# More turns between routing's top-k scans and around the recurrence's scan, in a two-layer macaron network with mixture of experts

## The chip, the cores and the metric

One core of a Trainium2 chip. The metric is the device time of one execution in microseconds (us), as the median of several executions. The profile is of one more execution.

## The reference, cut to what matters

The input is 16 sequences of 512 tokens with 128 channels. Six residual steps follow one another; each begins with a layer norm:

```
x = x + 0.5 * kan(norm(x))            # 64 inner units, each a sum of 16 relus
x = x + attention(norm(x))            # 16 heads of 8 channels, causal
x = x + 0.5 * kan(norm(x))
x = x + 0.5 * moe(norm(x))            # first pass over the experts, k = 0
x = x + recurrence(norm(x))
x = x + 0.5 * moe(norm(x))            # second pass, k = 1
```

The experts' step lets each of 8 experts choose its 128 best tokens of each sequence:

```
probs = softmax(x @ gate.T)                    # per token, over 8 experts
g, m  = top_k(probs of one sequence and expert over its 512 tokens, 128)
h     = gelu(x[m] @ w1[e]) @ w2[e]             # 128 -> 512 -> 128
out[m] += g * h
```

The recurrence is a gated linear scan over the 512 tokens with 64 states, `s = lam * s + u`, with `lam` from two sigmoids and `u` from a linear map of the normed input, and a linear map of the state and of the input back to 128 channels.

## The kernel before, in words

All residuals stay in on-chip memory (tiles `x0` to `x15`). The order of the instructions on TensorE (PE), VectorE (DVE), ScalarE (ACT) and GpSimd (POOL) is that of the program text as it runs: each engine takes its own instructions in that order and waits for what each needs. The text is a set of Python generators. One call of `turn()` advances every live generator to its next `yield`. So a `yield` means: let the others put their instructions in before mine go on. "A turn" below is one such round. It has no length of its own; it only fixes the order.

The first 1000 us are attention, the relu sums and the first scores, sequence by sequence. Then `hurry` is set, the pacing by budgets ends, and three things run beside one another:

- `experts()` (from L835) takes one job, a sequence and an expert, per three turns. A job's first product (`ps_h`, L879) stands in the first turn, its second (`ps_y`, L894) some turns later. For half of the experts the result is added back by a product with a selection matrix (`acc`, L912), which needs three DVE operations (L891, L903, L900); for the others GpSimd scatters it to memory (L926). If the next job's tokens have not been moved yet (`begun[0] < moved[0]` fails), the loop goes through its three turns without a new job.
- `fetch()` (L796) lets GpSimd gather the tokens of one job per turn (L805), in the order of `order`: 256 jobs, products and scatters mixed, of two passes. It stops at a job whose group of sequences has not been routed. `dispatch()` (L812) transposes gathered tokens on PE two jobs at a time (L827) and copies them.
- `recurrences()` waits until both sequences of a pair have come back from the first pass, then runs `recurrence(pair)` (L981): norms, transposes (L288), products, DVE's scan (L1010), the output products of both sequences (`leave`, L1017 and L1018), the residual add (L1023), and `gated(1, b)`, which norms again and computes scores (L692). A norm goes from DVE's statistics (L257, L261) to GpSimd's reciprocal root (L263, L264) back to DVE's normalisation (L274).

`routing(k, g)` (L700) starts when the eight sequences of group g have scores for pass k. It turns scores into probabilities, transposes them (L726), and then finds the 128 best of 512 for all 64 rows at once, eight per round: sixteen rounds of three DVE operations (`max` L738, `max_index` L740, `match_replace` L742). Each of these scans reads all 512 scores. After them the token numbers are converted and transposed (L749, L753, L754), copied (L756 to L758), and the group counts as routed. Of its four runs, (0,0) lies in the first 1000 us; (0,1), (1,0) and (1,1) run beside the experts. `if not hurry[0]` at L744 gives the first run three further turns after each scan; the others have one turn per scan.

The conditions that hold the gathers and the transposes:

```
while (k, g) not in routed or i >= moved[0] + 2 * E or ...:   # fetch
    yield
while i + 1 >= fetched[0] or i > begun[0] + AHEAD:            # dispatch, i even
    yield
```

Of the kernel before, what the change touches and what calls it, by code (L numbers as in the profile page):

```python
# [44 lines left out]
def tile_macaron(  # L45
# [51 lines left out]
    with ExitStack() as ph:  # L97
# [102 lines left out]
        def need(**work):  # L200
            while paced[0] and any(w > room[e] for e, w in work.items()):
                yield
            for e, w in work.items():
                room[e] -= w
# [10 lines left out]
        def rest(turns):  # L215

            for _ in range(turns if hurry[0] else 0):
                yield
# [3 lines left out]
        def bank(shape, dtype, name, work=0.0):  # L222


            while held[0] == 2 or (paced[0] and work > room["pe"]):
                yield
            room["pe"] -= work
            held[0] += 1
            return mm.tile(shape, dtype, name=name, tag="mm")

        def freed():
            held[0] -= 1

        def together(*gs):

            got, live = [None] * len(gs), list(enumerate(gs))
            while live:
                left = []
                for i, g in live:
                    try:  # L240
                        next(g)
                        left.append((i, g))
                    except StopIteration as end:
                        got[i] = end.value
                live = left
                if live:
                    yield
            return got
# [437 lines left out]
        def gated(k, b):  # L686

            xn, xT = yield from norm(x[b], whole=True)
            nc.sync.dma_start(out=xnd[b].rearrange("(c p) d -> p c d", p=P), in_=xn)
            ps = yield from bank([P, NT, E], F32, "ps_g", 0.9)  # L690
            for c in range(NT):
                nc.tensor.matmul(ps[:, c, :], lhsT=xT[:, bass.ts(c, P)], rhs=gateT, start=True, stop=True)  # L692
            yield
            take(dve=0.2)
            nc.vector.tensor_copy(scores[b // GB][:, :, b % GB, :], ps)
            freed()
            scored[k] += 1
            yield

        def routing(k, g):  # L700


            while scored[k] < (g + 1) * GB:
                yield
            N = GB * E
            sc3 = scores[g].rearrange("p c b e -> p (c b) e")
            mx = rtp.tile([P, NT * GB], F32, name="mx")
            probs = rtp.tile([P, NT, N], F32, name="probs")
            pr3 = probs.rearrange("p c (b e) -> p (c b) e", e=E)
            wide = [P, NT * GB, E]  # L710
            nc.vector.tensor_reduce(mx, sc3, AX.X, ALU.max)
            nc.vector.tensor_sub(pr3, sc3, mx.unsqueeze(2).to_broadcast(wide))
            yield
            nc.scalar.activation(pr3, pr3, AF.Exp)
            yield
            yield
            sm = rtp.tile([P, NT * GB], F32, name="sm")
            nc.vector.tensor_reduce(sm, pr3, AX.X, ALU.add)
            nc.vector.reciprocal(sm, sm)
            nc.vector.tensor_mul(pr3, pr3, sm.unsqueeze(2).to_broadcast(wide))  # L720
            yield
            yield
            yield from rest(2)
            ps = yield from bank([N, NT, P], F32, "ps_p")
            for c in range(NT):
                nc.tensor.transpose(ps[:, c, :], probs[:, c, :], ident)  # L726
            yield
            wk = rtp.tile([N, S], F32, name="wk")
            nc.vector.tensor_copy(wk, ps.rearrange("n c q -> n (c q)"))
            freed()  # L730
            gain = rtp.tile([N, CAP], F32, name="gain")
            tok = rtp.tile([N, CAP], U32, name="tok")
            for i in range(CAP // 8):
                m8 = gain[:, bass.ts(i, 8)]
                for op in range(3):
                    yield from need(dve=0.75)
                    if op == 0:
                        nc.vector.max(out=m8, in_=wk)  # L738
                    elif op == 1:
                        nc.vector.max_index(tok[:, bass.ts(i, 8)], m8, wk)  # L740
                    else:
                        nc.vector.match_replace(out=wk, in_to_replace=m8, in_values=wk, imm_value=-1.0)  # L742
                    yield
                    if not hurry[0]:  # L744
                        yield
                        yield
                        yield
            tokf = rtp.tile([N, CAP], F32, name="tokf")
            nc.vector.tensor_copy(tokf, tok)  # L749
            yield  # L750
            yield from rest(2)
            ps = yield from bank([P, 2, N], F32, "ps_r")
            nc.tensor.transpose(ps[:, 0, :], tokf, ident[0:N, 0:N])  # L753
            nc.tensor.transpose(ps[:, 1, :], gain, ident[0:N, 0:N])  # L754
            yield
            nc.vector.tensor_copy(tokI[g], ps[:, 0, :])  # L756
            nc.vector.tensor_copy(tokT[g], ps[:, 0, :])
            nc.vector.tensor_scalar_mul(gainT[g], ps[:, 1, :], 0.5)  # L758
            freed()
            routed.add((k, g))  # L760
            yield
# [219 lines left out]
        def recurrence(pair):  # L981
            half = [slice(a * M, (a + 1) * M) for a in range(2)]
            rows = (2 * pair, 2 * pair + 1)
            xTs = yield from together(*(norm(x[b], f"rope_{'ab'[a]}", w1p, True) for a, b in enumerate(rows)))
            xTs = [xT for _, xT in xTs]

            pf = yield from bank([P, S], F32, "ps_f")
            for a in range(2):
                nc.tensor.matmul(pf[half[a], :], lhsT=wf, rhs=xTs[a], start=True, stop=True)
            yield  # L990
            fg = w2p.tile([P, S], F32, name="fg", tag="kan_s")
            nc.scalar.activation(fg, pf, AF.Tanh, scale=0.5)
            freed()
# [3 lines that stand above are left out]
            pl = yield from bank([P, S], F32, "ps_l")  # L997
            nc.tensor.matmul(pl, lhsT=wlam, rhs=fg, start=True, stop=True)
            yield
            lam = w2p.tile([P, S], F32, name="lam", tag="oT")  # L1000
            nc.scalar.activation(lam, pl, AF.Tanh, bias=lbias, scale=0.25)
            freed()
            yield
            nc.vector.tensor_scalar(lam, lam, 0.5, 0.5, ALU.mult, ALU.add)
            pu = yield from bank([P, S], F32, "ps_u")
            for a in range(2):
                nc.tensor.matmul(pu[half[a], :], lhsT=wb, rhs=xTs[a], start=True, stop=True)
            yield
            s = w2p.tile([P, S], F32, name="s", tag="y")
            nc.vector.tensor_tensor_scan(s, lam, pu, 0.0, ALU.mult, ALU.add)  # L1010
            freed()
            yield

            def leave(a, b):
                po = yield from bank([P, NT, D], F32, "ps_h2")
                for c in range(NT):
                    nc.tensor.matmul(po[:, c, :], lhsT=xTs[a][:, bass.ts(c, P)], rhs=wx, start=True, stop=False)  # L1017
                    nc.tensor.matmul(po[:, c, :], lhsT=s[half[a], bass.ts(c, P)], rhs=wc[half[a], :],  # L1018
                                     start=False, stop=True)
                    if c == 1:  # L1020
                        yield
                yield
                nc.vector.tensor_add(x[b], po, x[b])  # L1023
                freed()
                yield
                yield from gated(1, b)

            yield from together(*(leave(a, b) for a, b in enumerate(rows)))

        def recurrences():  # L1030
            while scored[0] < B:
                yield
            for pair in range(B // 2):
                while done[0] < 2 * pair + 2:
                    yield
                yield from recurrence(pair)
# [128 lines left out]
```

## Time and profile before

| | us |
|---|---|
| median of 3 runs | 1751.41 |
| lowest, highest | 1749.4, 1756.8 |
| the profiled execution | 1746.91 |
| its span, first to last instruction | 1745.2 |
| mean granted clock of TensorE | 0.971 |
| routing's three scans of the 16 rounds, mean of one (L738, L740, L742) | 0.68, 0.68, 0.67 |
| the recurrence's scan (L1010), mean of one | 1.22 |
| an expert's gather on GpSimd (L805), mean of one | 0.98 |
| an expert's scatter on GpSimd (L926), mean of one | 1.62 |

The views: the page gives busy times of the engines over the whole span. A table of stretches gives the same for parts of it, with the clock that the throttle granted to TensorE. The timeline of one engine lists its instructions in order: start, duration, operation, output and inputs, and in brackets the idle time before it and who ended that. A row can merge several instructions of one kind; the time is then that of all. Ends of matrix products are modelled, so a busy TensorE is not one at full rate. Lines are those of the kernel before.

### The profile page before, as it was taken

What the parts mean: (1) busy time and instruction counts of PE and PEld (TensorE: products, weight loads), DVE (VectorE), ACT (ScalarE), POOL (GpSimd) and SP (SyncE); (2) the same over time, 40 slices, a digit from 0 to 9 for tenths busy, and PEclk for the clock granted to TensorE, in tenths of its full rate; (3) what the DMA queues carried; (4) which work ended last, traced back from release to release, by engine and by line L of the source; (5) the groups of instructions that cost most, each with busy time, mean ns of one, the idle gap of its engine ahead of it and who ended that gap; (6) DMA issues with size and microseconds to landing.
All of it is one profiled execution on the core that took longest, in us unless ns stands there. A gap on an engine that the chain in (4) does not pass through costs nothing. (4 is left out here: it accounts for less than half of the span.)

```text
span 1745.2 us, 35245 instructions
## 1 busy us (share of the span) xinstructions
PE 1636.9 (94%) x12879; PEld 1111.0 (64%) x12879; DVE 1107.3 (63%) x3604; ACT 996.6 (57%) x2000; POOL 977.6 (56%) x1453
## 2 busy tenths in 40 slices
PE   6788999999999999899899899999999999999997
PEld 2334444444444444444444389899988889989997
DVE  6677767777787788788876137643467444672222
ACT  3445667777777776677667654344443334444443
POOL 2524535545565455455534767567663777647773
PEclk9889999999999999999999899999998999999999
DMA  4211111011110111011122113233322233323342
GB/s 117 76 52 36 44 44 43 28 42 51 54 37 32 42 55 47 16 48 54 35 70 63 31 44 73 51 64 73 62 60 45 55 73 63 66 56 71 68 82 48
DMA packets 101753, 94.77 MB, mean 54 GB/s; under 512 B 11859, under 2 KB 90140, under 8 KB 101340
## 3 DMA queue, kind: packets, MB, share of 16 engines
q1 hardware_dynamic: 74512, 67.45, 12.5%
q0 software_dynamic: 26048, 24.93, 8.8%
q8 instruction: 101, 1.65, 0.4%
q14 instruction: 72, 0.59, 0.1%
q10 hardware_dynamic: 1020, 0.15, 0.0%
HBM read 58.93 MB, written 37.49 MB: 55 GB/s over the span
## 5 line engine op out<-in xcount | busy, mean ns | idle before, releaser
L625 ACT ACTIVATE pt<-ps_st 128x512 f32<-128x512 f32 (+1 forms) x704 | 386.9, 561 | 238.3 <-PE ps_st L622 232.9
L627 POOL TENSOR_SCALAR_AFFINE_SELECT pt<-pt 128x128 f32<-128x128 f32 (+2 forms) x704 | 247.0, 355 | 405.0 <-ACT pt L625 400.4
L569 DVE CUSTOM_DVE_ANT_0 below<-ps_sc,causal 128x512 bf16<-128x512 f32 (+1 forms) x512 | 316.5, 618 | 117.2 <-PE ps_sc L564 103.1
L881 ACT ACTIVATE mo<-ps_h 128x512 f32<-128x512 f32 x256 | 153.1, 598 | 262.2 <-PE ps_h L879 262.0
L805 POOL DMA_INDIRECT xg<-xnd,tokI x256 | 249.9, 976 | 80.5 <-issue 42.8
L879 PE MATMUL ps_h<-xin,mw 128*128 128x128 f32 x2048 | 281.1, 281 | 0.0
L894 PE MATMUL ps_y<-mw,mo 128*128 128x128 f32 x2048 | 274.7, 278 | 0.0
L564 PE MATMUL ps_sc<-kp,qp 72*128 72x512 bf16 (+3 forms) x1024 | 260.7, 307 | 10.6 <-DVE maxs L569 8.0
L622 PE MATMUL ps_st<-qp,kp 99*128 99x512 bf16 (+3 forms) x1024 | 259.8, 307 | 5.7 <-ACT pt L625 4.8
L879 PEld LDWEIGHTS ps_h<-xin,mw 128*128 128x128 f32 x2048 | 252.7, 194 | 6.3 <-issue 3.7
L926 POOL DMA_INDIRECT sum<-ye,tokI x124 | 201.3, 1624 | 97.7 <-ACT ye L897 31.2
L894 PEld LDWEIGHTS ps_y<-mw,mo 128*128 128x128 f32 x2048 | 251.7, 194 | 2.3 <-issue 1.0
L622 PEld LDWEIGHTS <-kp 99*128 99x128 bf16 x1024 | 94.2, 101 | 203.8 <-issue 185.4
L329 ACT ACTIVATE kan_h<-kan_s,rbias,kw 128x512 f32<-128x512 f32 x256 | 206.6, 814 | 7.1 <-PE ps_kg L335 6.9
L574 DVE TENSOR_REDUCE maxs<-ps_sc 128x2 f32<-128x512 f32 (+1 forms) x192 | 130.6, 685 | 70.5 <-PE ps_sc L564 69.3
L335 PE MATMUL ps_kg<-kan_h,w2d 128*64 128x512 f32 x512 | 164.7, 640 | 3.1 <-ACT kan_h L329 3.0
L645 PE MATMUL ps_av<-pt,va 128*32 128x512 f32 (+3 forms) x2048 | 166.8, 444 | 0.0
L564 PEld LDWEIGHTS <-qp 72*128 72x128 bf16 x1024 | 97.5, 100 | 55.6 <-issue 33.9
L900 DVE TENSOR_TENSOR mo<-mo 128x128 bf16<-128x128 f32 x132 | 38.3, 290 | 137.8 <-ACT mo L885 137.6
L912 PE MATMUL acc<-mo 128*128 128x128 bf16 x1584 | 113.0, 220 | 6.0 <-DVE mo L900 5.8
L912 PEld LDWEIGHTS <-mo 128*128 128x128 bf16 x1584 | 99.5, 99 | 23.8 <-issue 22.5
L645 PEld LDWEIGHTS ps_av<-pt,va 128*32 128x32 f32 x2048 | 53.6, 109 | 93.0 <-issue 49.7
(195 smaller groups left out, 2308.8 us busy)
## 6 DMA issues: line engine op xcount, KB each, us to landing
qp<-qs SPq DMA_DIRECT2D x64, 288.0 KB
xnd<-kan_x SPq DMA_DIRECT2D x32, 256.0 KB
sum<-x SPq DMA_DIRECT2D x31, 256.0 KB
qs<-qpart SPq DMA_DIRECT2D x48, 128.0 KB
kp<-ks SPq DMA_DIRECT2D x48, 96.0 KB
x<-in_L_attn_x_dram SPq DMA_DIRECT2D x16, 256.0 KB
mw<-in_L_ffn_w_dram SPq DMA_DIRECT2D x16, 256.0 KB
xg<-xnd,tokI POOLq DMA_INDIRECT x256, 2.5
```

The costliest lines, as they stand in the source:

```text
L329: nc.scalar.activation(h, sk, AF.Relu, bias=rbias[:, t : t + 1], scale=kw1[:, t : t + 1])
L564: nc.tensor.matmul(v[:, u, 0:n], lhsT=qp[r][0 : 9 * HD, g, bass.ts(c, P)], rhs=kp[0 : 9 * HD, r, 0:n], start=alone, stop=(u == len(gs) - 1 ...
L569: nc.vector.tensor_tensor_reduce(below[:, 0:n], v[:, 0, 0:n], causal[:, S - n : S], 1.0, LOWEST, ALU.add, ALU.max, accum_out=maxs[:, c, h ...
L622: nc.tensor.matmul(v[:, u, 0:n], lhsT=kp[ROWS, r, bass.ts(c, P)], rhs=qp[r][ROWS, g, c * P : S], start=True, stop=True)
L625: nc.scalar.activation(o, v[:, :, 0:n], AF.Exp, scale=HD ** -0.5)
L627: nc.gpsimd.affine_select(out=dg, in_=dg, compare_op=ALU.is_ge, fill=0.0, base=0, pattern=[[0, len(gs)], [1, P]], channel_multiplier=-1)
L645: nc.tensor.matmul(po[32 * g : 32 * g + 32, c * P : S], lhsT=va[:, c, r, :], rhs=pt[:, g, OFF[c] : OFF[c] + n], start=(c == 0), stop=(c == ...
L805: nc.gpsimd.indirect_dma_start(out=xgs[i // E % 2][:, i % E, :], out_offset=None, in_=xnd[b], in_offset=bass.IndirectOffsetOnAxis(ap=tokI[ ...
L879: nc.tensor.matmul(pst[:, f, :], lhsT=mw1[e][:, bass.ts(f, P)], rhs=xins[i // E % 2][:, i % E, :], start=True, stop=True)
L894: nc.tensor.matmul(py, lhsT=hs[u][:, f, :], rhs=mw2[e][:, f, :], start=(f == 0), stop=(f == NF - 1))
L912: nc.tensor.matmul(acc[:, c, :], lhsT=sels[u][:, bass.ts(c, P)], rhs=yes[u][:, w, :], start=(e == 0 and c == 0 and w == 0), stop=(e == las ...
L926: nc.gpsimd.indirect_dma_start(out=sums[k, b], out_offset=bass.IndirectOffsetOnAxis(ap=tokI[g][:, n : n + 1], axis=0), in_=ye[:, b % 2 * ( ...
```

## The change

Beside the experts, routing's first two scans of a round are followed by two turns each in place of one, the third by one as before: five turns for three scans. The recurrence gets one more turn before its product `ps_u`, two more after its scan, and one more after each sequence's residual add. Nothing is computed otherwise, and no tile or buffer changes.

```diff
@@ -744,6 +744,8 @@ routing
                     if not hurry[0]:
                         yield
                         yield
+                        yield
+                    elif op < 2:
                         yield
             tokf = rtp.tile([N, CAP], F32, name="tokf")
@@ -1002,6 +1004,7 @@ recurrence
             freed()
             yield
             nc.vector.tensor_scalar(lam, lam, 0.5, 0.5, ALU.mult, ALU.add)
+            yield
             pu = yield from bank([P, S], F32, "ps_u")
@@ -1009,6 +1012,9 @@
             nc.vector.tensor_tensor_scan(s, lam, pu, 0.0, ALU.mult, ALU.add)
             freed()
             yield
+
+            yield
+            yield
 
             def leave(a, b):
@@ -1022,6 +1028,7 @@
                 yield
                 nc.vector.tensor_add(x[b], po, x[b])
                 freed()
+                yield
                 yield
                 yield from gated(1, b)
```

## The prediction

> **What bounds the kernel now.** I read the page's busy shares first, then the table of stretches, then the timeline of single engines around the places where TensorE's share drops, and last the starts of each expert job.
>
> ```profile
> PE 1636.9 (94%) x12879; PEld 1111.0 (64%) x12879; DVE 1107.3 (63%) x3604; ACT 996.6 (57%) x2000; POOL 977.6 (56%) x1453
> ```
>
> TensorE is the bound. All edits take effect after 1000 us, beside the experts, so the question is where TensorE loses time there.
>
> ```profile
> 1060.00:1110.00 50.00, 44.88 (x414) 42.20 (x413) 47.62 (x141) 20.77 (x54) 32.40 (x30) 0.97 0.29 55
> 1325.00:1330.00 5.00, 5.00 (x19) 3.88 (x18) 0.62 (x1) 0.37 (x1) 0.00 (x0) 0.50 0.02 3
> 1500.00:1560.00 60.00, 56.96 (x561) 55.18 (x560) 49.10 (x135) 29.17 (x69) 33.13 (x28) 1.00 0.30 56
> 1575.00:1700.00 125.00, 125.00 (x1278) 124.66 (x1277) 35.77 (x105) 62.33 (x154) 97.42 (x83) 1.00 0.38 75
> ```
>
> Columns: stretch, its length, busy us of PE, PEld, DVE, ACT, POOL, granted clock, DMA share, GB/s. Without routing (last row) PE is full; with it (first, third row) DVE is full or nearly so and PE starves. In the second row PE counts as busy, but at half clock. The timeline of DVE and PE shows why:
>
> ```profile
> 1318.99 0.67 DVE L738 MAX8 gain<-wk 64x8 f32<-64x512 f32 x1
> 1319.59 1.19 DVE L1010 TENSOR_TENSOR_SCAN s<-lam,ps_u 128x512 f32<-128x512 f32 x1
> ```
>
> ```profile
> 1320.83 0.48 PE L1018 MATMUL ps_h<-wc,s 64*128 64x128 f32 x2 [1.91 <-DVE s L1010]
> ```
>
> The recurrence's scan stands behind routing's, its consumer is already next on PE, PE waits 1.91 us, and its clock is halved from 1322.5 to 1336.
>
> The first product of each job is a measure that half clock cannot hide. Every eighth job, in the timeline of PE:
>
> ```profile
> 1242.89 0.44 PE L879 MATMUL ps_h<-xin,mw 128*128 128x128 f32 x2
> 1264.92 0.44 PE L879 MATMUL ps_h<-xin,mw 128*128 128x128 f32 x2
> 1292.22 0.44 PE L879 MATMUL ps_h<-xin,mw 128*128 128x128 f32 x2
> 1317.59 0.44 PE L879 MATMUL ps_h<-xin,mw 128*128 128x128 f32 x2
> 1352.95 0.44 PE L879 MATMUL ps_h<-xin,mw 128*128 128x128 f32 x2
> ```
>
> These are jobs 80, 88, 96, 104 and 112. With a recurrence and no routing, eight jobs take 22.03 and the next eight 27.30 us; with routing 25.37 and 35.36. Experts alone: 18.06 (1586.83 to 1604.89).
>
> **The Trainium skill.** "TensorE: Matmul & The Clock Gate", Part 1, says that the clock falls to half after an idle window of about 3.4 us and comes back after a busy one. The trace agrees in kind: half clock lasts about 3.4 us after most gaps, but 13.65 us from 1322.5 on; even 1.98 us of waiting (at 1099.5) was enough. "DMA: Bandwidth & Descriptors", section on the SWDGE path, puts a fixed part of about 2.0 us on each transfer issued by GpSimd; the gathers here land 2.5 us after their issue (median), so I use 2.5.
>
> **Part 1: routing, what is won.** A block has 16 rounds of three scans. From 1307.73 to 1310.08 three scans and one 0.19 us operation went out, so a scan costs DVE 0.72 us. An expert job takes three turns. Three turns for three scans ask 2.16 us of DVE, beside some 0.5 for the job itself (0.75 for each second job's three operations, 0.4 for each fourth's copy, rounded up for the residual add) and, where a recurrence runs, about 0.76 (12.2 us per pair in 48 turns). PE needs 18.06/8 = 2.26 us without, 49.33/16 = 3.08 with a recurrence. So DVE is late by 0.3 to 0.4 us a job. With five turns DVE's share falls to about 1.8 of 2.26 and 2.6 of 3.08, and PE leads again.
>
> Loss against the undisturbed pace, from the job starts:
> - block (0,1), jobs 24 to 40 (1068.67, 1089.68, 1116.94): 21.01 - 18.06 + 27.26 - 22.03 = 8.2
> - block (1,0), jobs 96 to 120 (to 1376.65): 3.3 + 8.1 + (23.70 - 22.03) = 13.1, the wait for the scan and its half clock in it
> - block (1,1), jobs 160 to 184 (1508.78, 1528.71, 1549.67, 1568.77): 1.9 + 2.9 + 1.0 = 5.8
>
> That is 27; routing's own transposes, some 1.9, stay, which leaves 25. Bunches remain: eight statistics and eight normalisations put 2.2 and 2.1 us on DVE within five turns, and three or four of them fall into (1,0). I take 20 as won, bounds 14 and 25.
>
> **Part 2: the recurrence's turns.** They put one to two expert products between the scan and its consumer, which covers its 1.2 us. The gain is in the 13.1 already. In undisturbed pairs the scan ended before PE came to it (scan at 1165.70 for 1.22, consumer at 1167.53), so nothing is won there. Nothing is added but four turns until scores exist.
>
> **Part 3: what routing's delay costs.** A block's scans now need 80 turns, 26.7 jobs, in place of 48, 16 jobs. Following the generators turn by turn:
> - (0,1) starts after job 20 and ends near 48; job 59 is the first that needs it. Free.
> - (1,0) starts after job 98. Jobs from 122 on wait for it: 123 is the first of the second pass and tokens move in pairs. Before: 98 + 16 = 114, in time. After: 98 + 26.7 = 124.7, and four turns of tail: too late. Job 122 begins 15 turns late, five rounds of the expert loop issue nothing new.
> - (1,1) starts after job 162 or 163; jobs from 186 on wait. Before 178, after 190 and tail: again five empty rounds.
>
> An empty round is no fixed time: PE waits until DVE has finished, the gathers have been issued and landed.
>
> Dry spell 1, from the start of job 121's first product. Both halves of the recurrence's output (3.2 each, 1167.21 to 1170.44), a first product (0.95) and a second (0.9): x is added by 9.0. Behind that on DVE: four scans 2.9, statistics and aggregates 2.1, two expert operations 0.6 (GpSimd's two roots, 2.6, end about with them): 14.9. Normalisation 2.1, the last scan 0.75, conversions 0.4: 18.2. PE's last sum and the two small transposes: 19.1. DVE's residual add and token copy: 20. GpSimd issues the first gather 0.3 later, then one each 1.25 us:
>
> ```profile
> 1556.04 1.01 POOL L805 DMA_INDIRECT xg<-xnd,tokI  x1 [1.20 <-DVE gainT L758]
> 1557.35 1.05 POOL L805 DMA_INDIRECT xg<-xnd,tokI  x1 [0.30 <-PE ps_y L894]
> 1558.71 0.94 POOL L805 DMA_INDIRECT xg<-xnd,tokI  x1 [0.30 <-PE ps_x L827]
> ```
>
> The transposes of tokens 128 and 129 stand ahead of job 124: seven gathers, 20.3 + 7.5 + 2.5 = 30.3, job 124 at 30.6. In that time PE has 17.7 of work (recurrence 6.4, first products 2.9, second 2.7, sums 2.0, transposes 2.1, scores 1.7). Idle 12.9.
>
> Dry spell 2, from job 185. Seven scans 5.0 and 2.5 of expert and conversion work on DVE: 7.6; residual add and token copy 8.4; first gather 8.7, seventh lands at 18.7, job 188 at 19.1. PE's own work 8.7. Idle 10.4.
>
> After each, half clock for one to two windows costs 1.7 to 3.4; I take 2. Sum 14.9 + 12.4 = 27.3. Bounds 20 (DVE ahead of PE, a warm clock) and 38 (see below).
>
> One wait moves but stays: after (1,0) GpSimd works off its late gathers, and the next norm's roots stand behind them (a 2.56 us wait of PE at 1396.0, eight jobs in 32.88 for 27.30). After the change about 32 gathers, five scatters and two roots, 52 us, stand before the same norm of the next pair, which PE reaches at some 51: about the same wait. Counted at nothing, plus or minus 3. In spell 1 the gathers themselves are that queue. In (1,1) no norm follows.
>
> **Sum.** -20 + 27.3 = +7.3 us. The profiled execution took 1746.9 (span 1745.2), 4.5 below the median of 1751.4; so 1754.2 by its measure, 1758.7 by the median's.
>
> **Rivals.**
> - Not slower: the relief outweighs the dry spells. For it: DVE was over 95% busy in 1060 to 1110, so all of 25 may come back, and DVE may enter a dry spell ahead. Costs at their low end, 20: 1746; at best some 1742. Against it: both chains end in seven gathers in single file, which no faster DVE shortens. It decides where the spells together cost less than is won.
> - Clearly slower: the cold clock. If each spell is followed by 13.65 us of half clock, as at 1322.5, 6.8 in place of 2 is lost twice, and the norm's wait grows by 3: costs 38 to 40 and +18 to 20, 1770. Against it: that stretch was the recurrence's small products, while after the spells dense first and second products run.
>
> **Chances.** Forecast (+1 to +14) 0.55, 1752 to 1766 its own range; not slower 0.25, about half of it beyond 0.5%; clearly slower 0.20. Half a per cent, about what a measurement can tell from no change, is 8.8 us: faster 0.12; same 0.13 plus 0.32 of the forecast; slower 0.23 plus 0.20. Range 1744 to 1773, cutting a little from either rival.
>
> **What would show it.** Right: in the profile after, eight-job stretches of 18 and of 22 and 27 us where the scans run, no wait at the consumer of the scan, DVE below 90% there; two holes in PE of 10 to 13 us in all, one shortly before the first job of the second pass, one some 65 jobs later, each ended by a gather. Wrong: holes under 5 us, or eight-job stretches that keep their excess.

## The result, and the profile after

The median went from 1750.61 us (1746.59 to 1756.80, 20 runs) to 1757.61 us (1754.85 to 1760.54, 20 runs): a ratio of 1.0038, 95% interval 1.0030 to 1.0045, or +7.0 us for a forecast of +7.3. The profiled execution of after took 1758.35 (span 1756.6), so the two profiles are 11.4 apart in span. The profile of before was 3.7 below its kernel's median and that of after 0.7 above; the sums below are made on the two profiles and end on 11.4, not on 7.0. In after `ps_h` is L881, `ps_y` L896, `acc` L914, the gathers L807, their transposes L829, the recurrence's output L1023 and L1024.

The busy shares from the page of after:

```profile
PE 1640.2 (93%) x12879; PEld 1112.5 (63%) x12879; DVE 1108.6 (63%) x3604; ACT 1000.9 (57%) x2000; POOL 976.8 (56%) x1453
```

The work is the same to the instruction; only its order changed. From the table of stretches of after, the first and the third row for the two stretches shown of before, then the two places where scans have run out and the gathers are awaited (columns as before: stretch, length, busy us of PE, PEld, DVE, ACT, POOL, clock, DMA share, GB/s):

```profile
1060.00:1110.00 50.00, 50.00 (x488) 47.57 (x487) 43.09 (x127) 25.03 (x62) 36.71 (x34) 1.00 0.35 66
1375.00:1400.00 25.00, 18.04 (x111) 16.23 (x111) 12.88 (x62) 4.89 (x11) 16.04 (x19) 0.73 0.24 61
1500.00:1560.00 60.00, 59.40 (x597) 58.84 (x597) 41.60 (x117) 31.50 (x73) 33.45 (x27) 1.00 0.34 63
1570.00:1600.00 30.00, 23.15 (x191) 21.42 (x190) 10.62 (x33) 9.32 (x24) 20.14 (x20) 0.83 0.28 60
```

Where the scans run, PE is now full and DVE is at 86% and 69%, for 95% and 82% before. In their place stand two holes with idle time and a lowered clock. The timeline of PE through the first hole, cut to the rows that start after a wait and the first product of job 122:

```profile
1376.49 0.83 PE L914 MATMUL acc<-mo 128*128 128x128 bf16 x12
1380.53 2.37 PE L288 MATMUL ps_t<-ident,kan_x 128*128 128x128 f32 x8 [3.20 <-DVE kan_x L274]
...
1388.03 0.48 PE L829 MATMUL ps_x<-ident,xg 128*128 128x128 f32 x1 [3.23 <-DMA xg<-xnd,tokI]
1388.30 3.42 PE L692 MATMUL ps_g<-gateT,kan_xT 128*128 128x8 f32 x16
1391.58 1.84 PE L881 MATMUL ps_h<-xin,mw 128*128 128x128 f32 x7
```

And the second, in (1,1):

```profile
1579.63 0.48 PE L829 MATMUL ps_x<-ident,xg 128*128 128x128 f32 x1 [3.11 <-DMA xg<-xnd,tokI]
1581.05 0.45 PE L829 MATMUL ps_x<-ident,xg 128*128 128x128 f32 x1 [0.95 <-DMA xg<-xnd,tokI]
1582.13 0.47 PE L829 MATMUL ps_x<-ident,xg 128*128 128x128 f32 x1 [0.63 <-DMA xg<-xnd,tokI]
1582.40 1.92 PE L881 MATMUL ps_h<-xin,mw 128*128 128x128 f32 x8
```

In the first hole PE waits twice: 3.20 us for the norm of a recurrence's output, which without new expert jobs has nothing beside it to fill the time, then 3.23 us for the gather of the tokens that the late routing has only just named. In the second the waits shown are for gathers alone. The first gathers of the two holes, in GpSimd's timeline:

```profile
1385.31 1.03 POOL L807 DMA_INDIRECT xg<-xnd,tokI  x1 [2.46 <-DVE gainT L760]
1576.98 1.00 POOL L807 DMA_INDIRECT xg<-xnd,tokI  x1 [2.15 <-DVE gainT L760]
```

The job's first product at 1582.40 then runs at half clock: it takes 1.92, for 1.06 at 1568.42.

The starts of the first products give the account by stretches of jobs. (Below, "excess" is what a stretch takes over the undisturbed pace: 18.06 per eight jobs without a recurrence, 49.33 per sixteen with one.)

| jobs | us before | us after | difference | what happens there |
|---|---|---|---|---|
| 24 to 48 | 75.57 | 68.14 | -7.4 | scans of (0,1) |
| 48 to 64 | 49.33 | 56.02 | +6.7 | late gathers of (0,1) |
| 96 to 120 | 84.43 | 73.79 | -10.6 | scans of (1,0) |
| 120 to 144 | 82.80 | 98.30 | +15.5 | empty rounds of (1,0) |
| 160 to 184 | 59.99 | 55.23 | -4.8 | scans of (1,1) |
| 184 to 192 | 18.06 | 30.17 | +12.1 | empty rounds of (1,1) |
| before 24, and after the last | | | -1.5, +1.5 | |

All other stretches agree within 0.1 us. The sum is +11.5, by the unrounded numbers the 11.4 of the spans. The tail is what follows the last first product: 18.5 for 17.0. Of the -1.5 before job 24, 0.6 lies in jobs 16 to 24, where routing of (0,1) has begun, and is relief too.

### The profile page after: what moved, and what is told of

It reads as the page before. It is cut to its first block, busy times and chain, and to the rows that moved or that the text cites. A ratio compares the mean times of both kernels' runs of the same rounds, so it can differ in the third digit from the quotient of the medians.

```text
span 1756.6 us, 35232 instructions
## 1 busy us (share of the span) xinstructions
PE 1640.2 (93%) x12879; PEld 1112.5 (63%) x12879; DVE 1108.6 (63%) x3604; ACT 1000.9 (57%) x2000; POOL 976.8 (56%) x1453
## 3 DMA queue, kind: packets, MB, share of 16 engines
q1 hardware_dynamic: 74512, 67.45, 12.4%
## 5 line engine op out<-in xcount | busy, mean ns | idle before, releaser
L807 POOL DMA_INDIRECT xg<-xnd,tokI x256 | 249.1, 973 | 85.4 <-issue 45.8
L881 PE MATMUL ps_h<-xin,mw 128*128 128x128 f32 x2048 | 284.4, 283 | 0.0
L896 PE MATMUL ps_y<-mw,mo 128*128 128x128 f32 x2048 | 271.6, 276 | 0.0
L881 PEld LDWEIGHTS ps_h<-xin,mw 128*128 128x128 f32 x2048 | 256.1, 196 | 12.6 <-issue 9.9
L896 PEld LDWEIGHTS ps_y<-mw,mo 128*128 128x128 f32 x2048 | 250.2, 193 | 1.1 <-issue 0.8
L914 PE MATMUL acc<-mo 128*128 128x128 bf16 x1584 | 112.1, 220 | 1.5 <-DVE mo L893 0.5
L914 PEld LDWEIGHTS <-mo 128*128 128x128 bf16 x1584 | 99.7, 99 | 12.1 <-issue 9.2
```

The costliest lines, as they stand in the source:

```text
L807: nc.gpsimd.indirect_dma_start(out=xgs[i // E % 2][:, i % E, :], out_offset=None, in_=xnd[b], in_offset=bass.IndirectOffsetOnAxis(ap=tokI[ ...
L881: nc.tensor.matmul(pst[:, f, :], lhsT=mw1[e][:, bass.ts(f, P)], rhs=xins[i // E % 2][:, i % E, :], start=True, stop=True)
L896: nc.tensor.matmul(py, lhsT=hs[u][:, f, :], rhs=mw2[e][:, f, :], start=(f == 0), stop=(f == NF - 1))
L914: nc.tensor.matmul(acc[:, c, :], lhsT=sels[u][:, bass.ts(c, P)], rhs=yes[u][:, w, :], start=(e == 0 and c == 0 and w == 0), stop=(e == las ...
```

## The experiments

Three groups of kernels; those of a group ran on one chip, beside the kernel before. The chip of the first group ran the kernel before in 1783.91, those of the others in 1746.89 and 1746.64, so times are compared only within a group and by ratio. The edits are shown against the changed kernel, except that of the spread gathers in the kernel before.

**First group: the parts.** The recurrence's turns alone:

```diff
-                    elif op < 2:
-                        yield
```

> The changed kernel with only the recurrence's added turns; routing keeps three turns for three scans. My theory: the 7 us that the change costs come from routing being late, so this part alone costs nothing; it takes away the one wait for the recurrence's scan (1.91 us) and the 13.65 us of half clock after it (6.8 us): 5 to 9 us faster than before, about 1744. Rival, that the recurrence's turns delay the scores and so cause the loss: at or above 1751.

Measured: 1784.01, ratio 1.0008 (0.9994 to 1.0023). The expected 5 to 9 us are not won.

Routing's spacing alone:

```diff
-            yield
...
-            yield
-            yield
...
-                yield
```

> The kernel before with only routing's five turns for three scans. My theory: both dry spells are there (empty rounds of the expert loop at the same two places), so 4 to 9 us slower than before, 1755 to 1760, like the whole change. Rival, that the recurrence's turns cause the loss: 1735 to 1750.

Measured: 1811.65, ratio 1.0152 (1.0125 to 1.0180): 27.7 us slower, where 4 to 9 were expected. So the spacing is what costs; on this chip more than the whole change cost elsewhere. But the spacing also brings the relief without the recurrence's turns: jobs 96 to 120 take 72.55 us here, 73.79 in after, 81.24 with the recurrence's turns alone on this same chip. (The whole change was not run on this chip.) The profile has the holes of (1,0) and (1,1) here too, and 42.41 us for jobs 56 to 64, where the recurrence alone takes 27.30. A row of PE in that stretch:

```profile
1181.20 0.79 PE L1020 MATMUL ps_h<-wc,s 64*128 64x128 f32 x2 [5.00 <-issue]
```

PE has 5.00 us of idle time for which no semaphore shows a cause, while GpSimd issues gathers back to back. What that is stays open (below).

Four turns for three scans, so that routing ends before its first job is due:

```diff
-                    elif op < 2:
+                    elif op < 1:
```

> The changed kernel with four turns for three scans (64 turns, 21.3 jobs a block). My theory: DVE still gets room (three scans in four turns are 2.16 of 3.0 us), routing ends at job 121 and 185, just in time, so no round of the expert loop is empty: most of the 20 us of relief stays and the two dry spells shrink from 28 us to some 5 us of waiting for the first gathers: 8 to 15 us faster than before, 1736 to 1742. Rival, that DVE needs the five turns: within 4 us of before. Rival, that the holes are not due to lateness: about 1757.

Measured: 1797.93, ratio 1.0064 (1.0039 to 1.0089): slower, where 8 to 15 us were to be won. By the turn count no round of the expert loop is empty now (in (1,0) routing ends in turn 1187, due in 1190). Yet PE waits, as at the first gather of (1,0):

```profile
1379.78 0.48 PE L829 MATMUL ps_x<-ident,xg 128*128 128x128 f32 x1 [3.07 <-DMA xg<-xnd,tokI]
```

So to be in time by turns is not to be in time by us.

The change without the wait for routing in the second pass:

```diff
-                while (k, g) not in routed or i >= ...:
+                while (k == 0 and (k, g) not in routed) or i >= ...:
```

> The changed kernel, but the gathers of the second pass don't wait for its routing: they take the token numbers that stand in the buffer, so the second pass works in part on the first pass's tokens. All of routing's work and its five turns stay. My theory: both holes (15.5 and 12.1 us) vanish, as does the burst of late gathers: 25 to 33 us faster than the changed kernel, 1725 to 1733. Rival, that the holes come of DVE's work or of the clock and not of waiting for routing: 1750 or above.

Measured: 1763.12, ratio 0.9894 (0.9876 to 0.9913). This kernel computes something else, since the second pass takes in part the first pass's tokens; it serves to measure. With the same scans, turns and number of gathers, and the second pass's gathers no longer held back, it is 1.1% faster than before.

**Second group: the gathers in a burst.** First the changed kernel as a control.

> The changed kernel once more, as the control of these runs. Where the kernel before takes about 1750 us: 1.003 to 1.005 of it. Where it takes about 1784, as in the first four experiments: there TensorE waits while GpSimd works off late gathers, each matrix product on its own and for nothing that the profile names; the change makes two bursts of late gathers longer and adds one, so I expect 1.01 to 1.02 of it.

Measured: 1755.78, ratio 1.0057 (1.0039 to 1.0075), a little above what was expected.

The jobs 48 to 64 had not been forecast to cost anything. The timeline of GpSimd in after shows why they do. After a late routing of (0,1), gathers are issued back to back from 1139.39; the roots of the next norm stand behind them:

```profile
1177.44 0.95 POOL L807 DMA_INDIRECT xg<-xnd,tokI  x1 [0.30 <-PE ps_y L896]
1178.42 0.26 POOL L263 TENSOR_SCALAR ln_rstd<-ln_mv 128x4 f32<-128x4 f32 x1
1178.77 1.04 POOL L264 TENSOR_TENSOR ln_rstd<-ln_rstd,mhalf 128x4 f32<-128x4 f32 x1
```

The roots follow a gather without a pause. Their input had been there: DVE's timeline has it done at 1175.21, and at the norm ahead of this one, whose statistics are done at 1140.37, it is the same:

```profile
1139.74 0.63 DVE L261 BATCH_NORM_AGGREGATE ln_mv<-ln_st 128x2 f32<-128x6 f32 x8
1144.24 0.25 POOL L263 TENSOR_SCALAR ln_rstd<-ln_mv 128x4 f32<-128x4 f32 x1
1174.59 0.62 DVE L261 BATCH_NORM_AGGREGATE ln_mv<-ln_st 128x2 f32<-128x6 f32 x8
```

So the roots of the two norms come 3.9 and 3.2 us after their input, behind gathers; in the kernel before it is 1.2 and nothing. PE is then kept waiting for `kan_x`, 0.92 us at 1180.24, and runs at half clock from 1183.0 to 1186.4. Together this is the whole +6.7: the two norms' transposes hold PE for 1.9 and 2.7 us more than the 0.9 that each takes in before, the half clock costs 1.7, and routing's two small transposes, 0.4, which before stand in the stretch ahead (so 0.4 of the -7.4 there only moved). The test puts a turn between two gathers (`rest(1)` is a helper of the kernel that gives one turn):

```diff
                 fetched[0] += 1
                 yield
+                yield from rest(1)
```

> The changed kernel, with a gather each second turn instead of each turn (an expert job needs one in three turns). My theory of the queue: after a late routing fewer gathers and so fewer scatters stand before the norms' roots on GpSimd and fewer compete for the transfers; the two dry spells stay, since their first gathers come one after another anyway. 4 to 10 us faster than the changed kernel where the kernel before takes 1750, 15 or more where it takes 1784. Rival, that the burst costs nothing beside the dry spells: within 3 us of the changed kernel.

Measured: 1762.37, ratio 1.0090 (1.0073 to 1.0107): slower than the control, where 4 to 10 us were to be won. Jobs 48 to 64 take 49.77 us in this profile, nearly the undisturbed pace, for 53.37 in the control's and 56.02 in that of after. But jobs 64 to 72 rise from 22.01 to 24.48, where the backlog meets the next norm. Of the excess of (0,1) 1.1 to 3.8 come back in all, by one profile, and two profiles of the changed kernel are themselves 2.7 apart there. And jobs 120 to 128 take 46.46 (control 42.70) and 184 to 200 take 51.48 (48.15): where the first gathers are late already, to space them makes it worse.

Spread gathers with four turns for three scans:

```diff
-                    elif op < 2:
+                    elif op < 1:
...
+                yield from rest(1)
```

> The recurrence's turns, four turns for three scans, and a gather each second turn. My theory: no empty rounds, relief for DVE, a short queue: 15 to 22 us faster than before (0.987 to 0.992 of it). Rival, that four turns leave DVE the bound or that the first gathers still come late: within 8 us of before.

Measured: 1763.40, ratio 1.0097 (1.0077 to 1.0117), where 15 to 22 us were to be won. Jobs 120 to 128 take 48.51, the longest of the group, with no empty round. GpSimd's timeline shows it:

```profile
1370.39 0.95 POOL L807 DMA_INDIRECT xg<-xnd,tokI  x1 [0.31 <-issue]
1388.68 0.23 POOL L263 TENSOR_SCALAR ln_rstd<-ln_mv 128x4 f32<-128x4 f32 x1 [17.33 <-DVE ln_mv L261]
...
1391.55 1.08 POOL L807 DMA_INDIRECT xg<-xnd,tokI  x1 [0.18 <-issue]
```

and PE's, of the same kernel:

```profile
1394.17 0.48 PE L830 MATMUL ps_x<-ident,xg 128*128 128x128 f32 x1 [5.09 <-DMA xg<-xnd,tokI]
```

Now the gather stands behind the roots. GpSimd waits 17.33 us for statistics of a residual that PE has not finished, with a gather behind it that could have gone; PE then waits 5.09 us for that gather. In after it was the other way round. One queue in order holds both, so spacing one against the other only chooses which is late.

Spread gathers in the kernel before:

```diff
+                yield from rest(1)
```

> The kernel before with a gather each second turn. My theory: the queue ahead of the norm's roots after block (1,0) halves, so the 5.6 us that jobs 120 to 128 lost go: 4 to 7 us faster than before where that takes 1750; more where it takes 1784. Rival: the wait of that norm has another cause, and the time stays within 2 us.

Measured: 1745.15, ratio 0.9985 (0.9977 to 0.9993): 1.7 us are won, for 4 to 7 expected. Jobs 120 to 128 fall from 32.88 to 27.30, the undisturbed pace: the norm's wait after (1,0) was the burst. Jobs 128 to 136 rise from 22.62 to 26.82: the backlog reaches the next norm, where PE waits 1.46 us for the same `kan_x`.

**Third group: relief without lateness.** The changed kernel again.

> The changed kernel as the control of these four runs: 1.003 to 1.006 of before where that takes about 1750 us.

Measured: 1757.30, ratio 1.0069 (1.0056 to 1.0082), again a little above what was expected; span of the profile 1754.6.

The kernel of the first group without the wait for routing, on this chip:

> Once more the changed kernel whose second pass gathers by the token numbers that stand in the buffer, without waiting for its own routing (the second pass works in part on the first pass's tokens), now beside the changed kernel itself. My theory: both dry spells (15.5 and 12.1 us) go and no burst of gathers follows block (1,0) or (1,1), while the relief of DVE stays: 22 to 33 us faster than the control. Rival, that the holes come of DVE's work or of the clock: within 5 us of the control.

Measured: 1726.62, ratio 0.9884 (0.9868 to 0.9901): 30.7 us below the control. By the profiles (spans 25.6 apart) jobs 120 to 136 take 59.11 for 70.61, jobs 184 to 192 19.15 for 30.01, jobs 48 to 64 53.27 for 55.58, and the tail is 10.9 for 17.9 us. What is left in 120 to 136 has a 6.0 us wait of this kernel's own in it: routing may not write its token numbers before their early readers are done. The tail follows from scatters, which GpSimd has behind the gathers. The last ones of after:

```profile
1744.32 1.54 POOL L928 DMA_INDIRECT sum<-ye,tokI  x1 [2.48 <-ACT mo L887]
1748.23 1.54 POOL L928 DMA_INDIRECT sum<-ye,tokI  x1 [2.36 <-issue]
```

and the last one of this kernel:

```profile
1718.93 1.54 POOL L928 DMA_INDIRECT sum<-ye,tokI  x1 [2.75 <-ACT ye L899]
```

In after it comes 10.1 us after the last first product (1738.12), here 0.8 (1718.09). The kernel before has such a backlog too (8.9 us, tail 17.0), so only 0.9 to 1.5 of these 7 us of tail are what the change had cost.

The kernel with the recurrence's turns alone, again:

> Once more the recurrence's added turns alone, where the kernel before takes about 1750. In the first run of this kernel jobs 104 to 112, which hold the wait for the recurrence's scan and its half clock, took 30.16 in place of 35.36 us. My theory: 3 to 7 us faster than before. Rival: nothing is won, since the next norm's wait behind the gathers takes it up.

Measured: 1752.26, ratio 1.0036 (1.0022 to 1.0050). The expected gain is missed, and the rival of it holds. Jobs 104 to 112 take 30.25, 5.1 less than before; but 112 to 120 take 27.28 (+3.6) and 120 to 128 take 34.51 (+1.6). DVE stays behind by as much as before, and PE meets that a few rows later:

```profile
1323.88 0.48 PE L1022 MATMUL ps_h<-wc,s 64*128 64x128 f32 x2 [1.00 <-DVE s L1011]
1341.04 2.12 PE L288 MATMUL ps_t<-ident,kan_x 128*128 128x128 f32 x8 [0.47 <-DVE kan_x L274]
1360.54 0.27 PE L753 MATMUL ps_r<-ident,tokf 64*128 64x64 f32 x1 [3.09 <-DVE tokf L749]
```

The scan's wait is halved, and 3.09 us stand at the end of routing instead. The +0.36% itself does not lie there: in this profile jobs 0 to 255 take 1.1 us less than before, while the start is 3.4 and the tail 3.0 later.

A middle course: four turns for three scans in (0,1), and for the second pass one more turn in every second round alone:

```diff
-                    elif op < 2:
+                    elif op == 0 and (k == 0 or i % 2 == 0):
```

> The recurrence's turns; one more turn per round in block (0,1), one per second round in (1,0) and (1,1). So the second pass's routing ends 8 turns later than with the recurrence's turns alone, some 11 turns ahead of the job that needs it, where the changed kernel ends 14 turns after. My theory: about half of the relief (27 us at most) stays, no dry spell, no first gather is waited for: 6 to 14 us faster than before, so faster than both kernels. Rival, seen where routing ended just in time (four turns for three): the gathers still come too late, and the time is at or above before.

Measured: 1744.43, ratio 0.9994 (0.9984 to 1.0004): no difference to before that can be measured, where a gain was expected. Routing of (1,0) ends eleven turns ahead of its due turn. Jobs 24 to 48 take 68.77, nearly as in after. Yet 48 to 64 take 54.56, 112 to 120 take 30.30 and 176 to 184 take 22.76 (undisturbed 49.33, 22.03 and 18.06). In 112 to 120:

```profile
1366.10 0.33 PE L829 MATMUL ps_x<-ident,xg 128*128 128x128 f32 x1 [3.72 <-DMA xg<-xnd,tokI]
```

The job is not due yet; but `dispatch()` lays the transpose into PE's order as soon as the gather has been laid into GpSimd's, up to four jobs early (`AHEAD`), and PE, which is no longer slowed by DVE, comes to it 3.72 us before the data, for 0.92 in the kernel before. Behind it stand all other products.

## Why the prediction was right

The time lay in the range, and both main mechanisms, the relief of DVE and the two dry spells, were right. That the medians agree to 0.3 us is luck in part: one step failed by 6.7 us, and the two controls put the change at +8.9 and +10.7 us. By its steps:

- **Relief, 20 forecast.** 7.4 + 10.6 + 4.8 = 22.8, by blocks of the 27 that were lost: 7.4 of 8.2, 10.6 of 13.1, 4.8 of 5.8. In after the recurrence's scan ends at 1315.34 and its consumer starts at 1317.11 without a wait.
- **Part 2, the recurrence's turns.** They had no sum of their own, and alone they win nothing net in (1,0): 1.0008 (0.9994 to 1.0023) and 1.0036 (1.0022 to 1.0050). What was won of the 13.1 needed routing's spacing and, as far as the runs show, nothing else: the kernel with that spacing alone takes 72.55 for jobs 96 to 120, and its PE doesn't wait for the scan there. So the forecast's reason for these turns, to cover the scan's 1.2 us, was not needed once DVE had room.
- **Dry spell 1, 14.9.** From job 121's first product (1365.62) the first gather was forecast after 20.3 and job 124 after 30.6; they came after 19.7 (1385.31) and 31.6 (1397.20). The +15.5 of the stretch agrees with 14.9: over the undisturbed pace (76.63 for these 24 jobs) the excess was 6.2 before, the norm's wait and its half clock, and is 21.7 after. The wait moved and stayed, as forecast, 2.56 before and now at the next pair's norm:

```profile
1439.88 2.71 PE L288 MATMUL ps_t<-ident,kan_x 128*128 128x128 f32 x8 [3.17 <-DVE kan_x L274]
```

  The idle time and the clock are split otherwise than forecast: PE is counted busy for 24.6 of the 31.6 us, at a granted clock of 0.80, so 7.0 idle and not 12.9, and more of the loss is half clock than the 2 taken.
- **Dry spell 2, 12.4.** First gather forecast after 8.7, job 188 after 19.1; they came after 8.6 (1568.42 to 1576.98) and 19.5 (1587.88). Cost 12.1. "TensorE: Matmul & The Clock Gate" of the Trainium skill, Part 1, has the clock fall after an idle window of about 3.4 us; in after it is halved for 10.2 us from 1578.9, 2.4 us into the wait of 3.11. The trace agrees in kind, not in the figure: this wait, and the 1.91 us shown of before, were shorter and were followed by half clock all the same.
- **Part 3, "(0,1) ... Free".** This step failed: +6.7, put at nothing. Nothing was late for a job; the group's gathers were laid into GpSimd's queue later and closer together, in front of the roots of the norms, which the prediction had looked for after (1,0) alone. That the queue is the cause is shown by the 3.9 and 3.2 us that the roots come after their input, and by the spread gathers, with which the excess leaves jobs 48 to 64 and 2.5 us of it turn up at the next norm. In the sum it stands beside -22.8 for -20, +27.6 for +27.3, and -1.5 and +1.5 at the two ends: +11.4 for the forecast's +7.3. The medians say +7.0. So the forecast came closer to the medians than to its own kind of sum: the profiles are 4.4 further apart than the medians, which can't be laid to any stretch.
- **The rivals.** "Not slower" would have needed DVE well ahead at the spells; DVE's last scans came when forecast. "Clearly slower" needed 13.65 us of half clock after each. In the first spell half clock does last 3.4 and 10.2 us, 13.65 together, and in the second 10.2; but nearly all of it lies inside the spells, where PE waits for gathers anyway: after the starts of jobs 124 and 188 only 0.8 and 1.3 us of it are left.
- **The cause.** That most of the cost is the lateness in the second pass is shown by the kernel that doesn't wait there: 0.9884 (0.9868 to 0.9901) for 1.0069 (1.0056 to 1.0082). The rival that spacing slows the recurrence or the experts by itself falls with it. The cost in (0,1), where that kernel still waits for routing, stays: jobs 48 to 64 take 3.9 us over the undisturbed pace. Since in that kernel gathers also start sooner and lie less in bursts, the 30.7 us are the price of both, not of empty rounds alone.

What stays open: why the starts of job 0 lie up to 6.6 us apart between profiles (1001.4 to 1008.0) and the changed kernel takes 21.19 us for jobs 0 to 8 in one profile and 22.05 in another, while the program there is the same; and whether a version with gathers and roots on different queues would keep the relief. No version that computes the reference beat before by more than 0.15%.

## What to carry to other kernels

When a step is spread out to relieve an engine, count when it now ends and who needs its output, in the order of issue, and then in us: a job that is in time by turns can still find its data in flight. On an engine whose queue runs in order, a burst of issues is a wait for whatever small operation comes behind it, and a small operation that waits is a wait for all issues behind it. A wait taken from one consumer is won only if the engine that was late has less to do; otherwise it turns up at the next one. And try each part of a change alone: here routing's turns alone showed the relief and the cost, and no net gain from the recurrence's turns could be seen.

## What the runs showed of the hardware

In these traces gathers on GpSimd follow one another about every 1.25 us at the closest (0.95 and 0.30). At the end of the kernel the scatters of one sequence follow one another every 3.9 to 4.0 us (1740.30, 1744.32, 1748.23 in after), so a backlog of them can be read at the end of the span. On the chip of the first group PE stood up to 5.00 us with no cause that the profile shows while GpSimd issued gathers, and the same kernels' bursts cost more there: jobs 184 to 192 took 34.19 with the recurrence's turns alone, 18.06 on the other chip. It was not tried what does that.
